# Three-pass mean aggregation and a new engine order in a two-layer graph kernel

## The chip, the cores and the metric

The kernel runs on one core of one Trainium2 chip. The metric is the device time of one launch in microseconds (us). The core's five engines are TensorE (PE in the profile), VectorE (DVE), ScalarE (ACT), GpSimd (POOL) and SyncE (SP), which issues the DMA transfers. In the traces of this case each engine works through its instructions in the order of the program and waits at one whose inputs are not there yet (in e6 TensorE waits 2.50 us at one product). All runs below were in the fast state.

## The reference, cut to what matters

There are 128 independent graphs, each with 128 nodes, 512 features per node and a 128x128 adjacency matrix.

```python
# layer 0
h = max(layernorm(x), 0)
H = (adj != 0);  Dn = 1/(H @ adj[0]);  Be = 1/H.sum(over nodes)
r = layernorm(relu(Dn * H @ (Be * H.T @ (h @ W1.T)) + b1))     # 512 -> 1024
x = x + h + Dn * H @ (Be * H.T @ (r @ W2.T)) + b2              # 1024 -> 512
# layer 1
h = max(layernorm(x), 0)
agg = (adj @ h) / max(adj.sum(-1), eps)                        # mean aggregation
x = x + relu(concat(h, agg) @ W.T)
```

## The kernel before

The kernel is a software pipeline. One call of `step(s)` runs a part of graph `s + 2`, `s + 1`, `s` and so on down to `s - 3`, so that each engine always has work of several graphs. The 128 graphs give 128 steps. The first steps and a `head` fill the pipeline. The loop simply runs on past the last graph to empty it.

The weight products are done in float32r, each in three passes. A matrix is split into a high part h, a remainder l and a corrected part d, and the three products with the parts of the weights are summed in two PSUM banks (`pm`, `pd`). `low` and `rest` are where l and d are made.

```python
    def split_high(key, a, tags):
        ...
        copy(h, a, AF.Copy, scale=DOWN)                        # ScalarE
        def low(eng=nc.gpsimd):
            eng.tensor_tensor(SPLIT[key], a, h, SUB)           # two SBUF inputs
        def rest():
            nc.vector.scalar_tensor_tensor(t, h, 2.0**-12, low, MUL, SUB)   # two SBUF inputs
```

In the traces below, hh, hl and hd are these parts of layer 1's input, and nh, nl, nd those of r. The aggregation was one full fp32 product, placed between the main and the correction products of the second weights:

```python
    def aggregate(g):
        nc.tensor.matmul(OP[g][1], ANT.pop(g), GB.pop(g), start=False, stop=True, ...)

    def finish(g):
        o, pd = OP.pop(g)
        nc.vector.tensor_tensor(o, pd, o, ADD)
        nc.vector.scalar_tensor_tensor(X[g], o, 0.0, X[g], MAX, ADD)     # relu(o) + x
        nc.sync.dma_start(out=out[g], in_=X.pop(g))
```

A layer normalisation works in the same way three times per step. ScalarE sums, ScalarE sums the squares and takes the root, VectorE takes a reciprocal and a tiny product (`nm * rs`, 128x1), and ScalarE normalises. VectorE's tiny product has two SBUF inputs too. GpSimd does seven large operations per step: hl, nl, the additions of b1 in two halves, of c to g, and of h and b2 to x.

## Time and profile before

| Before | Value | From |
|---|---|---|
| time | 2546.71 us (2545.28 to 2549.6) | median of 4 runs, beside the changed kernel's |
| one step | 19.23 us | starts of the same product, step to step |
| TensorE busy in a step | 19.23 us, no gap | stretches view |
| VectorE, ScalarE, GpSimd busy in a step | 15.81, 14.39, 10.43 us | the same |
| step 4 starts at | 107.66 us | TensorE timeline |
| after step 127's products | 47.8 us | 2541.1 - 2493.3 (the prediction has 2493.1 and 48) |

A step is read between two starts of the same product, here rm, the first weights of layer 0. The prediction shows the lines of the page, the stretch and the timeline that carry this. Two more lines of before's VectorE timeline matter later (columns: start us, duration us, engine, line, operation, output <- inputs, partitions x elements, count):

```profile
1313.39 1.79 DVE L317 SCALAR_TENSOR_TENSOR z<-z 128x512 fp32r<-128x512 f32 x1
1319.52 0.69 DVE L505 SCALAR_TENSOR_TENSOR x_t<-o,x_t 128x512 f32<-128x512 f32 x1
```

The reader is to see that the last operation of a graph (relu(o) + x, line 505) takes 0.69 us here: GpSimd is idle beside it. The remainder of z is blocked to 1.79 us, but TensorE had other work then.

### The profile page before, as it was taken

The numbers are of one execution on the slowest core, as the hardware profiler recorded it, in microseconds if no ns is written. First come the engines' busy times: TensorE is split into PE (matmuls) and PEld (weight loads), VectorE is DVE, ScalarE is ACT, GpSimd is POOL, SyncE is SP. The second block draws the span as 40 slices with busy tenths as digits, with TensorE's granted clock in tenths as the row PEclk, the third lists the DMA queues.
The fourth block names the chain that finished last, engine by engine and source line by source line (L and its number), as shares of the span: only waits on it lengthen the run. The fifth ranks groups of instructions, "written<-read, shape, count | busy, mean of one in ns | idle before, by whom it ended". The sixth has DMA issues, their size and how long they took to land.

```text
span 2541.1 us, 38324 instructions
## 1 busy us (share of the span) xinstructions
PE 2490.4 (98%) x11024; PEld 1982.9 (78%) x11024; DVE 2057.7 (81%) x4523; ACT 1866.5 (73%) x3864; POOL 1324.0 (52%) x898
## 2 busy tenths in 40 slices
PE   6899999999999999999999999999999999999997
PEld 4687787877877877787787777878788788787875
DVE  7888888888888888888888878888887888888874
ACT  7677777777777777777777777777777777777773
POOL 2255555545545555554554555555455455555552
PEclk9899999999999999999999999999999999999998
DMA  6243344344344334434433433443443443344332
GB/s 171 86 130 121 119 128 127 117 129 128 116 127 127 118 120 128 126 118 129 128 114 128 127 118 119 129 126 117 129 128 113 125 131 119 120 129 125 117 124 74
DMA packets 409651, 311.70 MB, mean 123 GB/s; under 512 B 176736, under 2 KB 340576, under 8 KB 409440
## 3 DMA queue, kind: packets, MB, share of 16 engines
q1 hardware_dynamic: 408608, 309.18, 39.1%
q8 instruction: 87, 1.43, 0.2%
q14 instruction: 124, 1.02, 0.1%
q10 hardware_dynamic: 576, 0.07, 0.0%
q0 software_dynamic: 256, 0.01, 0.0%
HBM read 166.47 MB, written 142.61 MB: 122 GB/s over the span
## 4 chain that ended last, share of the span: by engine, by line
PE 94%; DMA 2%; DVE 1%; ACT 1%; issue 1%; POOL 1%; SPq 0%; DVEq 0%; POOLq 0%; ACTq 0%
PE gm L337 18%; PE rm L337 18%; PE bm L337 9%; PE am L337 9%; PE rd L343 9%; PE gd L343 9%; PE bd L343 4%; PE py L450 4%; PE ad L343 4%; PE pz L298 4%; PE ad L499 4%; PE ps_s L272 1%; DMA x_t<-in_x_dram 0%; DMA hb<-h_scratch 0%; DMA w11r<-in_w1t_dram 0%
## 5 line engine op out<-in xcount | busy, mean ns | idle before, releaser
L412 POOL TENSOR_TENSOR hl<-ht,hh 128x512 fp32r<-128x512 f32 x127 | 164.2, 1293 | 1019.8 <-ACT hh L408 524.6
L216 ACT ACTIVATE h<-x_t 128x512 f32<-128x512 f32 x256 | 161.5, 631 | 334.3 <-DVE x_t L453 318.0
L362 POOL TENSOR_TENSOR r<-r,b_bc 128x512 f32<-128x512 f32 x250 | 376.9, 1508 | 33.2 <-DVE r L361 33.2
L412 POOL TENSOR_TENSOR nl<-nt,nh 128x1024 fp32r<-128x1024 f32 x126 | 303.4, 2408 | 98.1 <-ACT nh L408 98.1
L356 ACT ACTIVATE r<-rm,dinv 128x512 f32<-128x512 f32 x256 | 174.8, 684 | 229.8 <-PE rm L337 229.8
L317 DVE SCALAR_TENSOR_TENSOR z<-z 128x512 fp32r<-128x512 f32 x128 | 227.4, 1777 | 4.4
L227 ACT ACTIVATE h<-x_t,rs 128x512 f32<-128x512 f32 x256 | 208.2, 813 | 12.0 <-DVE rs L223 7.8
L417 DVE SCALAR_TENSOR_TENSOR hd<-hh,hl 128x512 fp32r<-128x512 f32 x128 | 196.4, 1534 | 4.1 <-POOL hl L412 4.1
L314 DVE TENSOR_TENSOR z<-pz,z 128x512 fp32r<-128x512 f32 x128 | 88.5, 691 | 133.3 <-ACT z L310 133.3
L361 DVE SCALAR_TENSOR_TENSOR r<-rd,dinv,r 128x512 f32<-128x512 f32 x256 | 190.5, 744 | 5.5 <-ACT r L356 1.2
L343 PE MATMUL gd<-w20d,nd 128*128 128x512 f32 x512 | 189.3, 491 | 3.4 <-DVE nd L417 3.4
L210 ACT ACTIVATE h<-x_t,nm 128x512 f32<-128x512 f32 x256 | 185.4, 724 | 8.3
L298 PEld LDWEIGHTS pz<-s,h 128*128 128x128 f32 x1024 | 136.5, 195 | 65.6 <-issue 58.9
L293 POOL TENSOR_TENSOR x_t<-x_t,b_bc 128x512 f32<-128x512 f32 x128 | 168.2, 1314 | 20.4 <-DMA adjb<-in_adj_dram 10.5
L292 POOL TENSOR_TENSOR x_t<-x_t,h 128x512 f32<-128x512 f32 x128 | 164.1, 1282 | 27.8 <-ACT h L227 27.7
L222 DVE RECIPROCAL rs<-sd 128x1 f32<-128x1 f32 x384 | 58.7, 153 | 134.4 <-ACT sd L212 134.2
L227 ACT ACTIVATE r<-r,rs 128x1024 f32<-128x1024 f32 x128 | 158.9, 1241 | 6.3 <-DVE rs L223 1.9
L446 POOL TENSOR_TENSOR g<-g,c 128x512 f32<-128x512 f32 x126 | 162.6, 1291 | 0.0
L388 DVE STREAM_TRANSPOSE nt<-nb 128x1024 f32<-128x1024 f32 x128 | 157.6, 1232 | 5.8 <-DMA nb<-n_scratch 4.7
L337 PE MATMUL bm<-w30h,hh 128*128 128x512 f32 x512 | 154.1, 424 | 4.4 <-ACT hh L408 4.4
L417 DVE SCALAR_TENSOR_TENSOR nd<-nh,nl 128x1024 fp32r<-128x1024 f32 x128 | 154.7, 1209 | 2.7 <-POOL nl L412 2.7
L343 PEld LDWEIGHTS gd<-w20d,nd 128*128 128x128 f32 x512 | 96.3, 188 | 75.6 <-issue 31.0
(122 smaller groups left out, 6748.5 us busy)
## 6 DMA issues: line engine op xcount, KB each, us to landing
n_scratch<-r SPq DMA_DIRECT2D x128, 512.0 KB, 2.7
nb<-n_scratch SPq DMA_DIRECT2D x512, 128.0 KB, 2.7
x_t<-in_x_dram SPq DMA_DIRECT2D x128, 256.0 KB, 3.0
h_scratch<-h SPq DMA_DIRECT2D x128, 256.0 KB, 2.0
hb<-h_scratch SPq DMA_DIRECT2D x512, 64.0 KB, 2.0
out_dram<-x_t SPq DMA_DIRECT2D x128, 256.0 KB, 2.0
adj_t<-in_adj_dram SPq DMA_DIRECT2D x128, 64.0 KB, 1.8
an_scratch<-adj_t SPq DMA_DIRECT2D x128, 64.0 KB, 1.6
```

Source lines behind the costliest of these rows:

```text
L210: copy(junk, src, AF.Square, bias=NM[key], accum_out=ss)
L227: copy(dst, src, func, bias=rs[:, 1:2], scale=rs[:, 0:1])
L293: eng.tensor_tensor(X[g], X[g], b2_bc, ADD)
L298: nc.tensor.matmul(z[:, k * P : (k + 1) * P], H0[g][:, k * P : (k + 1) * P], S[g], start=True, stop=True)
L317: nc.vector.scalar_tensor_tensor(d, h, 2.0**-12, l, MUL, SUB)
L337: nc.tensor.matmul(pm, left[i](k), right(i, k), start=(i == 0 and k == 0), stop=(i == 1 and k == kk - 1))
L343: nc.tensor.matmul(pd, left[2](k), right(2, k), start=(k == 0), stop=(k == kk - 1), skip_group_check=True)
L356: copy(R[g][:, HALVES[half]], PY.pop((g, half)), AF.Copy, scale=DN[g][:, 1:2])
L361: nc.vector.scalar_tensor_tensor(r, PR.pop((g, half)), dn[:, 0:1], r, MUL, ADD)
L362: eng.tensor_tensor(r, r, b1_bc[:, cols], ADD)
L412: eng.tensor_tensor(SPLIT[key], a, h, SUB)
L417: nc.vector.scalar_tensor_tensor(t, h, 2.0**-12, low, MUL, SUB)
```

## The change

The intent, as the diff suggests: TensorE is the busiest engine, so its fp32 aggregation is made cheaper. The transposed mean operator (`anp`) and gb_t are split as the weights are, and three float32r products replace the fp32 one. The products with node matrices (ps_s, py, pz) stand together. The order of every engine in the step is new, and the last three steps are written out instead of running the loop on. The diff, cut to its core:

```diff
     def mean_transpose(g):
-        nc.vector.transpose(ANT[g], anb)
+        nc.vector.transpose(full, anb)
+        ANT[g] = h, l, d = [parts[:, i] for i in range(3)]
+        copy(h, full, AF.Copy, scale=DOWN / 4096.0)
+        def rest():
+            nc.vector.scalar_tensor_tensor(l, h, -4096.0, full, MUL, ADD)
+            nc.vector.scalar_tensor_tensor(d, h, -4097.0, full, MUL, ADD)
     def node_matrix(g):
-        copy(S[g], ps[:, :P], AF.Copy)
-        w = ps[:, P : P + 1]
+        copy(s, ps[:, : P + 1], AF.Copy)
+        DN[g] = s[:, P : P + 1]                  # w for dinv: from SBUF now, not PSUM
     def layer1_mean(g):
-        GB[g] = t = pool.tile([P, D], FP, tag="B", name="gb_t")
+        GB[g] = t = pool.tile([P, D], FP, tag="hbt", name="gb_t")     # shared with hb
+    def layer1_mean_high(g):
+        GB[g] = split_high(("b", g), GB[g], ("h2", "h3", "h1"))       # bh, bl, bd
     def aggregate(g):
-        nc.tensor.matmul(OP[g][1], ANT.pop(g), GB.pop(g), start=False, stop=True, ...)
+        for i, (left, right) in enumerate(zip(ANT.pop(g), GB.pop(g))):
+            nc.tensor.matmul(OP[g] if i == 2 else PY["o", g], left, right, ...)
     def finish(g):
-        nc.vector.tensor_tensor(o, pd, o, ADD)
-        nc.vector.scalar_tensor_tensor(X[g], o, 0.0, X[g], MAX, ADD)
+        nc.vector.scalar_tensor_tensor(o, o, 0.0, X.pop(g), MAX, ADD)
...
     def step(s, ...):          # new order, the parts that the argument touches
+        do(x_norm, s + 1)
+        do(residual, s + 1)                  # GpSimd: x+h0, x+b2
...
+        do(layer1_low, s - 3)                # hl, now VectorE
+        do(layer1_rest, s - 3)               # hd
+        do(inner_turn, s - 1)                # nt
+        do(inner_high, s - 1)                # nh
+        do(inner_low, s - 1)                 # nl, GpSimd
...
+        do(finish, s - 4)                    # o+x, a whole step later than before
+        do(layer1_spread, s - 2)
+        do(scales, s - 2, 3)
+        do(layer1_norm, s - 2)
+        do(layer1_mean_high, s - 3)          # bh
+        do(layer1_mean_low, s - 3)           # bl, GpSimd
+        do(inner_sums, s)                    # statistics of r
+        do(inner_rest, s - 1)                # nd
+        do(node_scale, s + 1)                # dinv
+        do(mean_rest, s - 3)                 # anp remainders
+        do(layer1_mean_rest, s - 3)          # bd
+        do(scales, s, 2)
+        do(inner_norm, s)
...
+        do(layer1_self, s - 3)
+        do(conv2_weights, s - 1)
+        do(aggregate, s - 3)
+        do(layer1_self_main, s - 3)          # o on ScalarE
...
-        for s in range(4, N + 3):
+        for s in range(4, N):
             step(s)
+        tail()
```

## The prediction

> **What bounds the kernel now.** I read the engine shares and the chain first, then one middle step in the timeline of each engine, then who blocks whom between VectorE and GpSimd. The page names TensorE:
>
> ```profile
> PE 2490.4 (98%) x11024; PEld 1982.9 (78%) x11024; DVE 2057.7 (81%) x4523; ACT 1866.5 (73%) x3864; POOL 1324.0 (52%) x898
> ...
> PE 94%; DMA 2%; DVE 1%; ACT 1%; issue 1%; POOL 1%; SPq 0%; DVEq 0%; POOLq 0%; ACTq 0%
> ```
>
> The columns are busy us, share and count; the second line is the chain that ended last, by engine. The same loop body runs once per graph, so the next view is one whole step, busy time by engine:
>
> ```profile
> 1301.06:1320.29 19.23, 19.23 (x88) 15.39 (x86) 15.81 (x36) 14.39 (x32) 10.43 (x7) 1.00 0.39 124
> ```
>
> After window and length come PE, PEld, DVE, ACT, POOL. TensorE has no gap in 19.23 us at full clock; VectorE has 3.4 us free, ScalarE 4.8. What the aggregation costs TensorE shows in starts (busy times overlap):
>
> ```profile
> 1317.61 1.02 PE L499 MATMUL ad<-gb_t,ant 128*128 128x512 f32 x2
> 1318.06 1.48 PE L343 MATMUL gd<-w20d,nd 128*128 128x512 f32 x4
> 1319.38 1.07 PE L343 MATMUL gd<-w21d,nd 128*128 128x512 f32 x4
> 1320.29 0.38 PE L272 MATMUL ps_s<-sb,adjt 128*128 128x129 f32 x2
> ```
>
> Four float32r products start 0.91 us apart as a group (1319.38 to 1320.29), 0.227 each. The fp32 aggregation and the group behind it take 1.77 (1317.61 to 1319.38), so the aggregation costs 0.86. Last, VectorE beside GpSimd:
>
> ```profile
> 1304.31 0.75 DVE L361 SCALAR_TENSOR_TENSOR r<-rd,dinv,r 128x512 f32<-128x512 f32 x1
> 1304.98 1.52 DVE L417 SCALAR_TENSOR_TENSOR hd<-hh,hl 128x512 fp32r<-128x512 f32 x1
> ```
>
> ```profile
> 1304.65 1.29 POOL L446 TENSOR_TENSOR g<-g,c 128x512 f32<-128x512 f32 x1
> 1305.91 1.72 POOL L362 TENSOR_TENSOR r<-r,b_bc 128x512 f32<-128x512 f32 x1
> ```
>
> hd reads two SBUF tiles. It starts while GpSimd adds g and ends 0.55 us after that add does (1306.50 against 1305.94); the next GpSimd add is longer by what it lost. r, which reads one operand from PSUM, isn't held up. The z remainder shows the same each step: 1.79 us beside the 2.40 us GpSimd subtraction nl, 0.69 free. The tiny scale product (128x1) too: once it met a GpSimd add with 0.62 us to go and took 0.64 instead of 0.16.
>
> **What the Trainium skill says.** "SBUF — State Buffer", section "SBUF: two separate sides": VectorE operations with two SBUF inputs, or in a two-port mode, share a port pair with GpSimd; it is held for a whole instruction and the loser fully blocks. The trace agrees (1.52 and 1.79 us above). "FP8 and Floating Point Precision", section "TensorE Precision Notes": true fp32 takes four passes. The trace agrees: 0.86 us is four times 0.215. "Perfetto Trace Analysis", section "Identifying the Most-Contended Engine", says to optimise the engine with the highest occupancy first; the change does so, and the question is whether it stays the right one.
>
> **The change part by part.**
> *TensorE.* The aggregation becomes three products of 0.227: 0.68 for 0.86, saving 0.18. ps_s, py and pz now follow one another; ps_s alone costs 0.26 now against 0.21 for four passes of 129 columns, so joining them gives at most 0.05. TensorE's work per step: 19.23 - 0.23 = 19.0.
> *VectorE* gains hl (0.69, from GpSimd), the remainder of the mean (0.69 as hd unblocked) and two 128x128 remainders (about 0.25 each): 15.8 + 1.9 = 17.7, if as much is blocked as now. *ScalarE* gains bh (0.6) and a 128x128 split (0.25): 15.2. GpSimd swaps hl for bl. All remain under 19.0, so shares alone promise 124 steps x 0.23 = 29 us, and the tail some more.
> *The order* decides otherwise. I followed the new order by hand, with durations and start-to-start times of this trace. Zero is ScalarE's start on o.
> - ScalarE: o and g main 1.04; the statistics of x 2.13 (3.17). g and ht on VectorE fit under it. Scales 0.4, then the norm starts at 3.60 and ends at 4.41. conv1's first main copy follows, ending at 5.00.
> - VectorE: r, first half, 5.04; hl ready at 5.71. GpSimd began x+h0 at 4.48 and holds the port to 5.76. hl gets in before x+b2, by about 0.1 us, and ends at 6.31. hd depends on hl; x+b2 takes the port first and keeps it to 7.60. hd ends at 8.15: 1.2 us blocked.
> - VectorE turns n, 8.07 to 9.30. ScalarE nh to 10.39. GpSimd nl 10.46 to 12.87. Meanwhile VectorE has 1.9 us of unblocked work and reaches o+x (two SBUF inputs) at 11.17: blocked to 12.87, done 13.42, that is 1.7 us lost.
> - z low; scales of layer 1, whose product meets the b1 add of GpSimd and ends at 14.70 (0.4 lost). ScalarE norm, bh, split of the mean to 16.13; statistics of r to 19.10. VectorE gb, ant, nd to 16.69; bl, held up by nd, ends at 17.94 and blocks the small remainders; bd is ready at 19.34.
> - Scales of r 19.62; r's norm 1.16; ScalarE reaches the next o at 20.8. VectorE, with z's remainder and the incidence (2.3), arrives at the same time.
>
> This is a closed chain from o to the next o, through ScalarE, VectorE and GpSimd, with no TensorE in it. It takes 20.8 us; without the blocked times it would take some 18.9, just under TensorE's 19.0. So I expect the steady step to rise from 19.23 to 20.8, TensorE idle for about 1.8 of it, mainly ahead of gd (waiting for nd) and bd.
> *Head and tail.* Step 4 starts on TensorE at 107.7 now; the new head does similar work, so I keep it. From the end of step 127's matmuls (2493.1) to the end it takes 48 us now, with waits of 3.64, 3.64 and 4.36 us ahead of py, py and bm and a cold clock. The written-out tail lets node 126's layer 1 run while node 127's exchange through DRAM is under way: an estimate of 40.
> *Sum:* 107.7 + 124 x 20.8 + 40 = 2727, plus the 5 us between span (2541) and median (2546): some 2730.
>
> **The rivals.**
> TensorE stays the bound: 19.0 a step, 107.7 + 2356 + 40 + 5 = 2509, 1.5% faster. For it: 100% busy now, all sums under 19.0, and an order that looks made to avoid some blocking (z's remainder now stands where GpSimd is idle). Against it: the chain would have to lose 1.8 us, as much as all its blocked time.
> hl loses its race for the port with x+b2. The margin is 0.1 us. Then hl and hd are both a GpSimd add later, 1.3 us a step: 22.1, about 2890.
> A transfer becomes the bound. hb and gb_t now share one buffer, so hb is loaded after bl. bl ends at 17.9, the load takes 2 to 3 us, and ht wants it 1.75 into the next step, at 22.6. r's single buffer is free 2.7 us after its norm, against a need at 4.3. Neither binds.
>
> **Range and chances.** If the chain holds but some collision falls out otherwise, a step takes 19.5 to 21.5, with the same head and tail 2570 to 2820. I put the middle a little under the sum, at 2710, since a blocked time left out is likelier than one overlooked. TensorE staying the bound gets nearly all of the rest, as the last steps and the head alone are worth about 10 us: mostly within 2%, or just over it if the tail gives more than I think.
>
> **What would show it.** Right: starts of rm 20.8 us apart in the middle; TensorE busy near 91%; the chain led by VectorE, ScalarE and GpSimd; hd near 1.8 us, o+x near 2.2, nd unblocked at 1.21, z's remainder near 0.7; the aggregation's three starts 0.23 apart. Wrong: TensorE still without a gap, o+x under 1 us, or a DMA as what ht, nt or r waits for. The prediction fails if GpSimd's subtraction nl and VectorE's o+x don't meet, for that removes 1.7 us from the chain at once.

## The result and the profile after

The changed kernel takes 2699.31 us (median of 4 runs, 2697.31 to 2701.17) against 2546.71 us. The ratio is 1.0598, with a 95% interval of 1.0579 to 1.0616. Ratios here are the mean time of one kernel's fast runs over that of the other's in the same rounds, so they are not quite the ratio of the medians quoted.

Where the 153 us came from is simple to see, because the steps are alike. Starts of rm, step 4 to step 127, are 123 intervals: (2625.27 - 107.06) / 123 = 20.47 us, against (2475.03 - 107.66) / 123 = 19.25 before. That is 1.22 us per step and 151 us over 124 steps. The head is 0.6 us shorter and the tail 3 us longer (2696.2 - 2645.2 = 51.0 us, against 47.8).

The page of the changed kernel, engine shares and then the chain that ended last, by engine ("issue" is time in which an engine waited for nothing that the profile shows, q marks an engine's sequencer):

```profile
PE 2544.0 (94%) x11152; PEld 1968.3 (73%) x11152; DVE 2403.7 (89%) x5037; ACT 1936.9 (72%) x4120; POOL 1479.4 (55%) x896
...
DVE 36%; ACT 31%; DMA 20%; issue 7%; SPq 4%; PE 1%; DVEq 0%; POOLq 0%; POOL 0%; ACTq 0%
```

TensorE still has the highest share, 94%, but it holds 1% of the chain that ended last, where it held 94%. VectorE and ScalarE lead the chain, and the transfers on it are r's way out to DRAM and back. GpSimd has 0% because what it costs is hidden in the length of the VectorE operations that it blocks. The transfers don't set the step here: before the transposition nt, which needs r back as nb, VectorE waits for nb 0.2 us in all from step 4 on. In the step shown below nb landed at about 1302.7, 0.9 us before nt starts, and VectorE was in hd until then. The page's chain follows the transfer all the same. So r's way through DRAM is a second loop, less than 1 us shorter than the one through VectorE's queue. The TensorE timeline over one step shows where TensorE stands still:

```profile
1312.15 1.20 PE L353 MATMUL gd<-w20d,nd 128*128 128x512 f32 x4 [0.83 <-DVE inv L289]
1313.19 1.08 PE L353 MATMUL gd<-w21d,nd 128*128 128x512 f32 x4
1314.11 0.39 PE L522 MATMUL am<-bh,anp 128*128 128x512 f32 x1
1314.34 0.40 PE L522 MATMUL am<-bl,anp 128*128 128x512 f32 x1
1314.57 0.44 PE L522 MATMUL ad<-bd,anp 128*128 128x512 f32 x1
1314.85 1.09 PE L349 MATMUL rm<-w10h,z 128*128 128x512 f32 x4
...
1335.32 0.86 PE L349 MATMUL rm<-w10h,z 128*128 128x512 f32 x3
```

The bracket is the idle time just before an instruction and what ended it. The three products start 0.23 us apart, as intended. TensorE waits 0.83 us for nd (VectorE's inv is the instruction that follows nd). That wait doesn't set the step: nd is late because VectorE is. The VectorE timeline of the same step:

```profile
1301.34 0.68 DVE L423 TENSOR_TENSOR hl<-ht,hh 128x512 fp32r<-128x512 f32 x1
1302.05 1.66 DVE L428 SCALAR_TENSOR_TENSOR hd<-hh,hl 128x512 fp32r<-128x512 f32 x1
...
1306.68 2.32 DVE L531 SCALAR_TENSOR_TENSOR o<-o,x_t 128x512 f32<-128x512 f32 x1
1308.92 0.68 DVE L326 TENSOR_TENSOR z<-pz,z 128x512 fp32r<-128x512 f32 x1
1309.52 0.15 DVE L217 RECIPROCAL st<-st 128x1 f32<-128x1 f32 x1
1309.70 0.47 DVE L218 TENSOR_TENSOR st<-st 128x1 f32<-128x1 f32 x1
...
1312.39 0.87 DVE L292 SCALAR_TENSOR_TENSOR dinv<-s,inv 128x1 f32<-128x1 f32 x1
...
1314.66 0.16 DVE L217 RECIPROCAL st<-st 128x1 f32<-128x1 f32 x1 [0.20 <-ACT st L213]
```

And GpSimd beside it:

```profile
1301.49 1.67 POOL L305 TENSOR_TENSOR x_t<-x_t,b_bc 128x512 f32<-128x512 f32 x1
...
1306.04 2.41 POOL L423 TENSOR_TENSOR nl<-nt,nh 128x1024 fp32r<-128x1024 f32 x1 [1.17 <-ACT nh L419]
1308.41 1.75 POOL L372 TENSOR_TENSOR r<-r,b_bc 128x512 f32<-128x512 f32 x1
1311.62 1.62 POOL L423 TENSOR_TENSOR bl<-gb_t,bh 128x512 fp32r<-128x512 f32 x1 [1.47 <-ACT bh L419]
```

The two are read together. o+x starts at 1306.68, while nl runs to 1308.45 (1306.04 + 2.41), and ends at 1309.00, 0.55 us after nl. Before it took 0.69 us, so 1.63 us of its 2.32 are blocked. hd ends 0.55 us after x+b2 (1303.71 against 1303.16): 0.97 us blocked. The tiny product of the scales ends 0.01 us after the addition of b1 (0.47 instead of 0.16), and dinv 0.02 us after bl (0.87 instead of 0.16). This agrees with what the Trainium skill says on the page "SBUF — State Buffer", section "SBUF: two separate sides": the pair of ports is locked for a whole instruction.

That the loss recurs in every step shows in the groups of the page (count, then busy us in total and mean ns of one):

```profile
L531 DVE SCALAR_TENSOR_TENSOR o<-o,x_t 128x512 f32<-128x512 f32 x128 | 290.1, 2267 | 0.1
...
L428 DVE SCALAR_TENSOR_TENSOR hd<-hh,hl 128x512 fp32r<-128x512 f32 x128 | 209.5, 1637 | 4.4
```

ScalarE closes the loop. Its timeline:

```profile
1295.74 0.57 ACT L517 ACTIVATE o<-am 128x512 f32<-128x512 f32 x1
...
1304.90 1.06 ACT L419 ACTIVATE nh<-nt 128x1024 fp32r<-128x1024 f32 x1 [3.52 <-DVE nt L400]
...
1310.21 0.82 ACT L222 ACTIVATE h<-x_t,st 128x512 f32<-128x512 f32 x1 [1.33 <-DVE st L218]
...
1316.20 0.58 ACT L517 ACTIVATE o<-am 128x512 f32<-128x512 f32 x1
```

ScalarE waits 3.52 us for VectorE's nt (late because of hd) and 1.33 us for the scales (late because of o+x). It then does the statistics of r and reaches the next o 20.46 us after the last one.

### The profile page after: what moved, and what is told of

Read it like the earlier page. It is cut to its first block, busy times and chain, and to the rows that moved or that the text cites. A ratio compares the mean times of both kernels' runs of the same rounds, so it can differ in the third digit from the quotient of the medians.

```text
span 2696.2 us, 39610 instructions
## 1 busy us (share of the span) xinstructions
PE 2544.0 (94%) x11152; PEld 1968.3 (73%) x11152; DVE 2403.7 (89%) x5037; ACT 1936.9 (72%) x4120; POOL 1479.4 (55%) x896
## 3 DMA queue, kind: packets, MB, share of 16 engines
q8 instruction: 88, 1.44, 0.2%
q14 instruction: 132, 1.08, 0.1%
## 4 chain that ended last, share of the span: by engine, by line
DVE 36%; ACT 31%; DMA 20%; issue 7%; SPq 4%; PE 1%; DVEq 0%; POOLq 0%; POOL 0%; ACTq 0%
DVE o L531 10%; DMA nb<-n_scratch 10%; DMA n_scratch<-r 9%; ACT r L222 6%; DVE nt L400 6%; ACT junk L212 6%; ACT r L207 5%; DVE r L371 4%; SPq L393 4%; DVE st L218 3%; DVE x_t L464 3%; ACT h L222 3%; ACT bh L419 3%; DVE o L527 3%; DVE z L326 3%
## 5 line engine op out<-in xcount | busy, mean ns | idle before, releaser
L419 ACT ACTIVATE nh<-nt 128x1024 fp32r<-128x1024 f32 x128 | 135.9, 1061 | 451.6 <-DVE nt L400 451.6
L372 POOL TENSOR_TENSOR r<-r,b_bc 128x512 f32<-128x512 f32 x250 | 435.9, 1744 | 28.8 <-DMA anb<-an_scratch 27.3
L222 ACT ACTIVATE h<-x_t,st 128x512 f32<-128x512 f32 x256 | 208.8, 816 | 168.5 <-DVE st L218 168.5
L423 POOL TENSOR_TENSOR bl<-gb_t,bh 128x512 fp32r<-128x512 f32 x126 | 204.4, 1622 | 197.4 <-ACT bh L419 195.9
L531 DVE SCALAR_TENSOR_TENSOR o<-o,x_t 128x512 f32<-128x512 f32 x128 | 290.1, 2267 | 0.1
L353 PE MATMUL gd<-w20d,nd 128*128 128x512 f32 x512 | 152.8, 420 | 106.4 <-DVE inv L289 94.3
L305 POOL TENSOR_TENSOR x_t<-x_t,b_bc 128x512 f32<-128x512 f32 x128 | 214.7, 1677 | 21.0 <-DMA adjb<-in_adj_dram 11.1
L222 ACT ACTIVATE r<-r,st 128x1024 f32<-128x1024 f32 x128 | 159.4, 1245 | 55.5 <-DVE st L218 55.5
L212 ACT ACTIVATE h<-x_t,st 128x512 f32<-128x512 f32 x256 | 184.6, 721 | 4.3
L217 DVE RECIPROCAL st<-st 128x1 f32<-128x1 f32 x384 | 60.9, 159 | 120.6 <-ACT st L213 120.5
L353 PE MATMUL bd<-w30d,hd 128*128 128x512 f32 x512 | 154.0, 422 | 2.3 <-DVE w30d L122 2.3
```

What stands on the lines that cost most here:

```text
L212: copy(junk, src, AF.Square, bias=t[:, 1:2], accum_out=t[:, 2:3])
L222: copy(dst, src, func, bias=t[:, 5:6], scale=t[:, 4:5])
L305: eng.tensor_tensor(X[g], X[g], b2_bc, ADD)
L353: nc.tensor.matmul(pd, left[2](k), right(2, k), start=(k == 0), stop=(k == kk - 1), skip_group_check=True)
L372: eng.tensor_tensor(r, r, b1_bc[:, cols], ADD)
L531: nc.vector.scalar_tensor_tensor(o, o, 0.0, X.pop(g), MAX, ADD)
```

## The experiments

Eleven kernels ran, all with correct results and in three rounds or more beside the kernel before. "us per step" is the mean of the 123 intervals described above, from the profiled run. By the 2% measure e9 is the same as the kernel before, e7 is unclear, and all others are slower.

| Run | What differs | Median us | Ratio to before, 95% interval | us per step |
|---|---|---|---|---|
| before | | 2546.71 | 1 | 19.25 |
| after | the change | 2699.31 | 1.0598 (1.0579 to 1.0616) | 20.47 |
| e1 | after, scale product with one input | 2680.96 | 1.0526 (1.0510 to 1.0542) | 20.34 |
| e2 | after, o+x off VectorE | 2650.97 | 1.0408 (1.0392 to 1.0424) | 20.08 |
| e3 | e1 and e2 | 2615.21 | 1.0266 (1.0249 to 1.0283) | 19.79 |
| e4 | new order, old aggregation | 2763.28 | 1.0847 (1.0831 to 1.0863) | 21.01 |
| e5 | e4, gb_t not in hb's buffer | 2617.32 | 1.0280 (1.0265 to 1.0296) | 19.84 |
| e6 | old order, three passes | 3097.61 | 1.2166 (1.2148 to 1.2185) | 23.67 |
| e7 | e3, all known collisions apart | 2596.23 | 1.0195 (1.0178 to 1.0212) | 19.68 |
| e8 | e6, placed with more care | 2933.06 | 1.1522 (1.1505 to 1.1539) | 22.33 |
| e9 | e7, x+b2 earlier | 2542.07 | 0.9979 (0.9973 to 0.9986) | 19.23 |
| e10 | after, without the written-out tail | 2700.16 | 1.0609 (1.0593 to 1.0624) | 20.48 |
| e11 | after, dinv with one input | 2696.19 | 1.0591 (1.0573 to 1.0609) | 20.47 |

The theory was that the new order forms a chain through ScalarE, VectorE and GpSimd that is lengthened by waits for the shared ports. The rivals were that VectorE's occupancy (89%) is what counts, that the three passes' splitting costs the time, and that the chain is one of plain dependences.

### e1: the scale product with one tensor input

```diff
-        nc.vector.tensor_tensor(t[:, 5:6], t[:, 1:2], t[:, 4:5], MUL)
+        nc.vector.tensor_scalar(t[:, 5:6], t[:, 1:2], t[:, 4:5], None, MUL)
```

> The changed kernel, with the 128x1 product of the layer norm scales (mean times reciprocal) written as an operation with one SBUF tensor and a pointer scalar, so that it no longer needs the port shared with GpSimd; nothing else moves. Theory (a closed chain through ScalarE, VectorE and GpSimd, with every blocked time on it): the product no longer waits the 0.31 us for GpSimd's b1 add, 0.47 becomes 0.16 us each step, and the step falls from 20.46 to some 20.15 us, about 2661 us in all. Rival (VectorE's added work binds, the blocked times are incidental): no change, 2699 us. Rival (TensorE's own work binds): no change.

VectorE's timeline shows that the form with a pointer is no longer blocked beside the addition of b1:

```profile
1302.17 0.21 DVE L218 TENSOR_SCALAR st<-st 128x1 f32<-128x1 f32 x1
```

It takes 0.21 us each time, where the two-input form took 0.16 unblocked. There are three such products on the chain. One falls from 0.47 to 0.21, and two rise from 0.16 to 0.21: -0.26 + 0.05 + 0.05 = -0.16 us per step expected from these durations, and 0.13 measured. The gain is real but was put too high before the run, because the longer form had been left out.

### e2: o+x off VectorE

The relu of o goes to ScalarE, the addition to GpSimd ahead of nl, and o's correction to the end of the step before.

```diff
+        do(finish_relu, s - 4)      # copy(o, o, AF.Relu), behind conv1_main(s, 1)
...
         do(inner_high, s - 1)
+        do(finish, s - 4)           # nc.gpsimd.tensor_tensor(o, o, x, ADD)
         do(inner_low, s - 1)
...
-        do(layer1_self_out, s - 4)
-        do(finish, s - 4)           # scalar_tensor_tensor on VectorE
```

> The changed kernel, with the last addition o+x taken off VectorE: the addition from PSUM moves to the end of the step before, where VectorE waits, ScalarE applies the relu where it waits for n, and GpSimd adds x ahead of its subtraction nl. VectorE loses 2.3 us a step of which 1.77 were blocked. Rival (VectorE's occupancy of 89% binds): the step falls to TensorE's 19.0 us, about 2518 us. Theory (closed chain): what stood behind o+x then meets the next blocked time, since the scale product waits for the b1 add of GpSimd that now starts right behind nl; the step falls by 0.3 us alone, to 20.15, about 2661 us. GpSimd's longer list could take 0.1 us of it back.

The rival of occupancy is falsified: VectorE lost 1.9 us of busy time per step ((2403.7 - 2163.0) / 124), more than the 1.5 by which the step exceeds TensorE's 19.0, and the time is nowhere near 2518 us. The theory's own number was right only in sum, and the trace shows a new wait:

```profile
1306.57 0.16 DVE L217 RECIPROCAL st<-st 128x1 f32<-128x1 f32 x1 [1.75 <-ACT st L213]
1306.76 0.65 DVE L218 TENSOR_TENSOR st<-st 128x1 f32<-128x1 f32 x1
```

VectorE now waits 1.75 us for ScalarE's root, and the scale product is blocked for 0.49 us instead of 0.31. From nt to this reciprocal it took 5.88 us in the changed kernel (1303.64 to 1309.52) and 5.29 here (1301.28 to 1306.57). So 0.59 us are saved, less 0.18 by the scale product: 0.41, against 0.39 per step measured. The rest of the 2.32 us of o+x turned into waiting, because ScalarE's way from nt to the root is only 0.59 us shorter than VectorE's was.

### e3: both

Both edits together.

> Both edits, the one-input scale product and o+x off VectorE. Theory: with both blocked times gone, the chain from nl to the norm of layer 1 waits for ScalarE's own statistics instead; the norm starts 0.9 us earlier and the step is 19.6 us, about 2595 us: more than the two edits' 0.3 us each together. If the edits only add up: 19.85 us, 2623 us. Rival (occupancy): as with the second edit alone.

Alone, the edits give 0.13 and 0.39 us per step, together 0.68. The 0.16 more follows from e2: with o+x gone, the scale product was blocked for 0.49, so making it one-input is worth 0.18 more there. The two edits hold each other's gain. Still, 19.79 us is more than the 19.6 expected. VectorE still waits 1.75 us for ScalarE's root.

### e4 and e5: the new order with the old aggregation

The splits of gb_t and of the mean operator are taken out, and one fp32 product stands where the three were. In e5, gb_t goes back to the buffer that it had before:

```diff
-        GB[g] = t = pool.tile([P, D], FP, tag="hbt", name="gb_t")
+        GB[g] = t = pool.tile([P, D], FP, tag="B", name="gb_t")
```

> The changed kernel with the aggregation put back to one fp32 product: no split of the mean nor of its operand, all of the new order and tail kept. Theory: ScalarE loses bh and the split of the mean (0.7 us) from the chain, GpSimd's bl no longer blocks VectorE; the chain takes some 19.75 us a step, about 2611 us, still slower than the 2547 us before: the new order costs by itself. Rival (the added splitting work is the whole cause): TensorE binds again at 19.2 us, about 2543 us.

> The new order with the old aggregation (one full-precision product, no splitting of gb_t and of the mean operator), and gb_t in a buffer that hb does not share, which the run with the new order alone lacked. Without bh, bl, bd and the two anp remainders VectorE loses about 1.5 us and ScalarE about 1 us of work per step, but most of it does not stand on the chain from o to the next o: bd (0.7) and the remainders of the mean operator do. Theory (the new order's chain through ScalarE, VectorE and GpSimd with o+x blocked by nl sets the step): about 19.75 us per step, 2611 us, still above the kernel before, which has the same products. Rival (the splitting of the aggregation costs the time, the order is harmless): TensorE binds at 19.2, 2543 us. If hb still comes late and VectorE still waits for it, 20.5 or more, 2720 us, and the buffer was not the cause.

e4 was a miss: less work, and slower than the change. VectorE's waits from step 4 on (total us, times, longest) say why:

```profile
DVE ht L391 <- DMA hb<-h_scratch: 168.9, 119, 2.7
```

hb and gb_t share one buffer. With three passes gb_t is free after bl, but as fp32 it is read by TensorE at the very end of the step, and hb is loaded only then. This is the prediction's rival of the transfer, which didn't bind in the changed kernel (the same wait there is 1.5 us in all) and does here. e5 takes this away and meets the theory's number: 2617.32 us for 2611. So the new order alone costs 19.84 - 19.25 = 0.59 us per step with the same products on TensorE, and the rival (2543 us) falls. The three passes add another 0.63 (20.47 - 19.84). The trace suggests why, without a run of its own: ScalarE's bh and split of the mean stand between the norm of layer 1 and the statistics of r, which start 1.44 us after the norm in the changed kernel (1310.21 to 1311.65) and 0.72 after it in e5. VectorE's part, bd and the remainders, which the expectation put on the chain, is not on it: VectorE waits 0.20 us for ScalarE after bd.

### e6 and e8: three passes in the old order

e6 takes the kernel before and adds the three passes. bh stands behind gb_t, the remainders and bd ahead of the second weights, and the products behind them. e8 moves these.

```diff
 # e6                                       # e8
         do(layer1_mean_out, s - 3)
+        do(layer1_mean_high, s - 3)        # behind inner_sums(s)
+        do(layer1_mean_low, s - 3)         # behind inner_sums(s)
         do(layer1_self, s - 3)
         do(inner_sums, s)
         do(inner_rest, s - 1)
...
         do(inner_out, s)
+        do(mean_rest, s - 3)               # behind inner_rest(s - 1)
+        do(layer1_mean_rest, s - 3)
-            conv2_weights(s - 1, between)
+        do(conv2_weights, s - 1)
+        do(aggregate, s - 3)
+        do(layer1_self_main, s - 3)        # behind scales(s + 2, 1)
```

> The kernel before, in its old order, with the aggregation alone changed to three passes (bh, bl, bd and the split mean operator added; the three products stand behind the second weights' products of the same step). Theory (the order made the time worse, not the passes): TensorE still binds, and loses the 0.86 us product for three of 0.23, so 0.1 to 0.2 us less per step, 2520 to 2547 us, if the splits find room in the idle time of VectorE (3.4 us per step) and ScalarE (4.8); TensorE may wait somewhat for bd, up to 2600. Rival (the passes' own splitting costs the time): about 20.4 us per step, 2690 us.

> The three passes alone in the old order again, with the faults of the first try mended: bh stands behind the statistics of r on ScalarE (there it waited 2.05 us for gb_t in front of them), the two remainders of the mean operator stand right behind nd on VectorE (there behind the scales of r and the sparse operands, 2.5 us after TensorE wanted them), and the copy of o stands behind the sums of the next x. By the old step's times: bh ends some 0.6 us behind the statistics of r, bl 1.3 to 1.5 later, bd 0.7 later, about when the last product of the second weights ends. Theory (placement on in-order engines decides, not the work): 19.1 to 19.6 us per step, 2530 to 2595 us. Rival (three passes do not fit in this step at any place, because bh, bl, bd is a chain of three engines that starts only when gb_t is there): over 21 us per step, over 2770 us.

Both missed by far. The TensorE timeline of e6, and one stretch of it (window, length, then busy us of PE, PEld, DVE, ACT, POOL, granted clock, DMA share, GB/s):

```profile
1316.67 0.40 PE L522 MATMUL am<-bh,anp 128*128 128x512 f32 x1
1319.57 0.77 PE L522 MATMUL am<-bl,anp 128*128 128x512 f32 x1 [2.50 <-DVE anp L260]
1320.28 0.80 PE L522 MATMUL ad<-bd,anp 128*128 128x512 f32 x1
```

```profile
1319.50:1321.20 1.70, 1.63 (x5) 1.11 (x5) 0.76 (x3) 0.83 (x2) 0.00 (x0) 0.50 0.83 327
```

VectorE reaches the remainders of the mean operator late, as they stand behind the scales of r and the sparse operands. TensorE waits 2.50 us, and after that its granted clock is 0.50 for about 3.4 us: the next four products of rm take 1.79 us from start to start instead of 0.91. From bl to the second products of rm (`rm<-w10l`) it takes 3.37 us here, but 2.20 in the 17 of 123 steps that stay at full clock, so the clock adds some 1.2 us to the wait. The count nearly closes: 2.67 us more to bl (2.90 instead of 0.23), 0.84 more for the two products after it (0.71 + 0.59 instead of 2 x 0.23), 0.88 more for rm, 4.39 in all, on 19.03 makes 23.4, against 23.67. The Trainium skill, page "TensorE: Matmul & The Clock Gate", section "HAM oscillation — how this bites in real kernels", gives the rule "no PE-idle gaps >~3.4µs". Here some 2.5 us of idling was enough in most steps. The length of the gap alone doesn't decide it: of the 17 steps at full clock, seven had gaps of 2.41 to 2.53 us.

e8 mends this and runs at full clock (0.992), but has two other waits of TensorE, here in total from step 4 on:

```profile
PE ad L522 <- DVE bd L430: 173.1, 123, 1.5
PE py L463 <- POOL g L459: 153.2, 125, 5.8
```

bd is late because VectorE's tiny scale product ahead of it meets the bl that has just begun, and takes 1.16 us instead of 0.16:

```profile
1314.35 1.16 DVE L223 TENSOR_TENSOR rs<-nm,rs 128x1 f32<-128x1 f32 x1
```

g is late because ScalarE's main copy of g waits 1.48 us for the finish of the graph before. The total came out where the rival put it (over 2770 us), but not by the chain of three engines that it named alone: in this trace it is one more collision at the port, and a wait that my placement made. Whether three passes fit into the old order at another place is left open. What the two runs show is that they don't drop into it. A new order for them was needed, and the change's own is better than either of these.

### e11: dinv with one input

dinv's w was moved from PSUM to SBUF by the change, so dinv has had two SBUF inputs since. The prediction didn't list this collision, of 0.71 us per step.

```diff
-        nc.vector.scalar_tensor_tensor(dn[:, 0:1], w, 0.0, inv, ALU.is_gt, MUL)
+        nc.vector.tensor_scalar(dn[:, 0:1], w, 0.0, inv, ALU.is_gt, MUL)
```

> The changed kernel with dinv alone in the one-input form (inv as a pointer), so that it no longer waits for GpSimd's bl: 0.87 us becomes 0.21. The prediction's list of blocked operations did not have it. Theory (only what stands on the chain counts): in the changed kernel VectorE waits 0.20 us after bd for ScalarE's statistics of r anyway, and those do not wait for dinv, so the 0.66 us saved turn into waiting: 20.46 us per step as before, 2692 to 2702 us. Rival (all blocked time of VectorE counts, as it is the busiest engine): 124 x 0.66 = 82 us less, 2617 us.

The step stays at 20.47 us. The 3 us between the medians are, in the profiled runs, in the head (step 4 starts at 103.88 instead of 107.06). VectorE's timeline shows where the time went:

```profile
1308.61 0.21 DVE L292 TENSOR_SCALAR dinv<-s,inv 128x1 f32<-128x1 f32 x1
...
1308.93 0.69 DVE L255 SCALAR_TENSOR_TENSOR anp<-anp,ant 128x128 fp32r<-128x128 f32 x1
...
1310.88 0.16 DVE L217 RECIPROCAL st<-st 128x1 f32<-128x1 f32 x1 [0.45 <-ACT st L213]
```

The wait for bl's lock moved to the next operation with two inputs (anp, 0.69 us instead of 0.28), and the rest became waiting for ScalarE's root (0.45 instead of 0.20). Blocked time off the chain is worth nothing.

### e7 and e9: keeping the two sides apart

e7 is e3 with dinv as in e11, x+b2 moved behind bl so that it does not come between hl and hd, hl and hd ahead of r's first half, the small operations of the mean operator moved away from the front of the normalisation, and nl behind the second half of the addition of b1. So it moves more than the blocked operations. e9 moves x+b2 once more, to right behind x+h0, where VectorE's operations have at most one SBUF input.

```diff
 # e9 against e7
         do(residual_add, s + 1)
+        do(residual_bias, s + 1)            # x+b2
...
         do(layer1_mean_low, s - 3)
-        do(residual_bias, s + 1)
```

> The changed kernel with every two-input VectorE operation of the chain either moved or made one-input, so that none meets a GpSimd addition: relu of o on ScalarE and +x on GpSimd, scale product and dinv with the scale as a pointer, x+b2 behind nl and bl so that it does not come between hl and hd, the mean operator's small operations away from the front of the normalisation. Theory (port blocking and the order of waits make the chain longer than TensorE's work): no chain is longer than 19.0 us, TensorE binds, 107 + 124 x 19.0 + 52 + 3 = 2518 us, faster than both kernels; VectorE's clashes with x+b2 may leave up to 19.3, 2555 us. Rival (the chain is one of plain dependences, blocking adds little): no better than the run with both earlier changes, 19.74 per step, 2615 us.

> The version with both sides of the port kept apart, with x+b2 moved on GpSimd from behind bl to right behind x+h0. In the run before, the two remainders of the mean operator were blocked there (0.69 and 1.38 us against 0.28 unblocked) and bd came 0.25 us too late for TensorE. Theory (that blocking sets the 19.67 us per step still left): the remainders end about 1 us earlier, r is normalised 0.6 us earlier, 19.0 to 19.2 us per step, 2515 to 2540 us, level with or just under the kernel before. Rival (the way of r through DRAM, its norm, and the next transposition is a loop of its own): 19.5 to 19.7, 2575 to 2600 us.

e7 fell between the theory (2518) and its rival (2615). VectorE's timeline showed that x+b2 had only found another victim, the second remainder of the mean operator, with bd behind it:

```profile
1305.81 1.38 DVE L264 SCALAR_TENSOR_TENSOR anp<-anp,ant 128x128 fp32r<-128x128 f32 x1
1307.11 0.68 DVE L442 SCALAR_TENSOR_TENSOR bd<-bh,bl 128x512 fp32r<-128x512 f32 x1
```

In e9 that remainder takes 0.28 us, and the page reads as before's did, shares and then chain:

```profile
PE 2486.7 (98%) x11152; PEld 2000.7 (79%) x11152; DVE 1972.7 (78%) x4913; ACT 2019.0 (79%) x4244; POOL 1529.0 (60%) x1020
...
PE 89%; ACT 3%; DMA 2%; DVE 2%; POOL 2%; issue 1%; SPq 1%; POOLq 0%; DVEq 0%; ACTq 0%
```

TensorE is the bound again. Its quickest step takes 19.03 us (the median 19.15), which is the 19.0 that the prediction worked out for the three passes. The mean is 19.23, because some steps are longer, eight of the 123 over 19.75. In one of these, VectorE waited 2.80 us for r's way back from DRAM, against 1.90 in a step of 19.06, and TensorE then 0.95 for nl:

```profile
584.43 1.20 PE L363 MATMUL gm<-w20l,nl 128*128 128x512 f32 x4 [0.95 <-POOL nl L437]
```

VectorE waits for r's way back in nearly every step (204.6 us in all from step 4 on), so the loop that e9's rival named is the next one behind TensorE's work.

So e9 is 157 us faster than the changed kernel and level with the one before: 0.2% faster (20 and 23 runs), too little to be called a gain in practice. At 2542.07 us it lies just outside its theory's 2515 to 2540, and far from its rival's 2575 to 2600.

### e10: without the written-out tail

```diff
-        for s in range(4, N):
+        for s in range(4, N + 4):
             step(s)
-        tail()
```

> The changed kernel with the written-out last three steps taken away: the loop runs on through four emptier steps instead, as in the kernel before. The steps of the middle are untouched (20.46 us). The prediction took 40 us for the written-out tail and the trace shows about 51 from the last product of step 127 to the end. If writing it out helps as the change intends, this run is slower by 5 to 25 us: 2705 to 2725 us. If it is neutral or worse, 2690 to 2700 us.

2700.16 us against 2699.31: neutral, within the scatter of the runs. From the end of step 127's products to the end it takes 51.8 us (2698.4 - 2646.6), and written out 51.0. The written-out tail has its own waits of TensorE, 4.47 us ahead of py and 3.34 ahead of bm, of the kind that it was to remove.

## Why the prediction was right, and where it was not

It said 2710 us and "slower", with a sum of 2730. Measured are 2699. By its terms:

- **The bound changes.** Right, and it is the point that decided. A chain from o to the next o through ScalarE, VectorE and GpSimd sets the step (the chain view: TensorE 1%), not the busiest engine. The Trainium skill, page "Perfetto Trace Analysis", section "Identifying the Most-Contended Engine", goes by the highest occupancy, but judges TensorE by its weight loads rather than by matmul time. By these (73%) it would name VectorE (89%), which leads the chain with 36%. But e2 shows that VectorE's share doesn't set the time either.
- **The step of 20.8 us.** Measured 20.47. Each point on the way came a little earlier, counted from ScalarE's o: the norm starts at 3.51 (3.60 predicted), hd ends at 7.97 (8.15), o+x at 13.26 (13.42), the scale product at 14.43 (14.70), the scales of r at 19.27 (19.62). The collisions on this way were the predicted ones. The last leg was not: the prediction had bl block the small remainders and bd end last, at 19.34, ahead of the scales of r. In the trace bl blocks dinv instead, bd ends at 18.72, and ScalarE's statistics of r at 18.88, so ScalarE closes the loop. In all the size was off by 0.33 us, 41 us in 124 steps.
- **The collisions.** hl won the race for the port in the changed kernel (0.68 us), hd and o+x were blocked as described (means 1.64 and 2.27 us; 1.8 and 2.2 predicted), the z remainder (0.69) and nd (1.18) were free. dinv was missed, and e11 shows that it costs nothing.
- **Without the blocked times some 18.9, under TensorE's work.** The prediction's own losses come to 3.3 us (1.2, 1.7 and 0.4), of which it takes off 1.9 without saying what then holds the rest. The step of e9, bound by TensorE with a quickest step of 19.03, agrees, and it confirms TensorE's 19.0. But e9 needed other moves than unblocking, so it doesn't measure the 18.9.
- **TensorE busy near 91%.** Wrong: 94% over the span and 19.64 of 20.47 us in a step. A product after a wait is recorded longer here (gd 1.20 us, the next group 1.08), so the share doesn't fall as far as the waiting rises. The starts are what to read. TensorE waited ahead of gd as predicted, but not ahead of bd.
- **The tail, 40 us.** This is the term of the sum that was mis-sized most by proportion: 51.0 us. The overlap that the estimate counted on brought less than a microsecond (e10). The errors of the step and of the tail partly cancel: -41 + 11, and with the head (-0.6) and the distance from span to median (3 instead of 5) the sum (2732 before rounding) becomes 2699. That the stated 2710 came so near is partly luck: 20 us were taken off the sum by judgement, on the view that a predicted collision may fail to happen.
- **"For that removes 1.7 us from the chain at once."** Wrong. e2 keeps nl and o+x apart and gains 0.39 us per step, as ScalarE's statistics stood only 0.59 us behind, and the scale product's blocking grew. A loop through three engines has parallel branches, and the second longest limits what the longest can give.
- **"Neither binds"**, on the shared buffer of hb and gb_t. Right for the change. e4 shows that it holds only because the three passes release gb_t early.

## What to carry to other kernels

When a change lightens the busiest engine, write down the loops that close through the other engines' in-order queues and compare their length with that engine's work: the longest loop sets the step, whatever the shares say. On such a loop, list every VectorE operation with two SBUF inputs, however small, beside every GpSimd operation that can run then. Remove collisions one by one and re-read the trace after each, since a wait that is taken away may land on the next such operation (e7, e11) or on the next branch (e2).

## What the Trainium skill lacked or had wrong

- "SBUF — State Buffer" gives the lock, but not who gets it next. Here a waiting VectorE operation got in between two GpSimd operations queued back to back (o+x, which ends 0.55 us after nl, ahead of the addition of b1), while between two dependent VectorE operations GpSimd got in (x+b2 between hl and hd, in every step).
- The same page has no figure for how late a blocked VectorE operation ends. By these traces it ends after the GpSimd operation by 0.55 us for 512 elements per partition, 0.14 to 0.15 for 128, and 0.01 to 0.02 for one. A 128x1 product can lose 1.00 us (e8, 1.16 instead of 0.16), and the form with a pointer for its second input was never seen blocked (0.21 to 0.22 us each time between 110 and 2500 us in e1, e3, e7, e9 and e11).
- "TensorE: Matmul & The Clock Gate" warns of idle gaps over some 3.4 us. In e6 gaps of about 2.5 us brought the granted clock to 0.50 for up to 3.4 us in most steps, and to 0.93 over the span, while in 17 of 123 steps, seven of them with gaps of 2.41 to 2.53 us, it stayed at 1.00. After gaps of 1.4 and 1.5 us (e8) the clock was 0.992 over the span.
- "Perfetto Trace Analysis" ranks engines by occupancy, and TensorE by its weight loads or its share of the peak rate (not computed here). By weight loads, the kernel before has VectorE ahead (81% against 78%), though TensorE had no gap in a step and 94% of the chain. In the changed kernel VectorE leads by more (89% against 73%), and e2 took 1.9 us per step off it for a gain of 0.39.
